# A convolution-and-attention chain on one core: three of 24 depthwise chains move to TensorE

## The chip, the cores and the metric

The kernel runs on one core of one Trainium2 chip. The metric is the device time of one execution in microseconds (us). Every time below comes from runs of the kernel before the change: three timed runs, and one execution that the hardware profiler recorded.

## The reference

Four layers run one after the other on x of shape (4, 256, 64, 64), float32, each on a group-normalised input and added to its own input. Layer 0 is a deformable convolution with a feed-forward part, layer 2 a 3x3 convolution with binarised weights, layer 3 a non-local attention block with 2x2 max pooling. The change lies in layer 1, a linear attention with a depthwise 5x5 convolution:

```python
qkv = relu(conv1x1(x, qkv_w) * qkv_bn_scale + qkv_bn_bias)       # 768 channels
agg = depthwise5x5(qkv, agg_dw_w) + agg_dw_b                      # 768 channels, 25 taps each
agg = agg * agg_pw_w + agg_pw_b                                   # per channel
t = concat([qkv, agg]) split into heads of q, k, v (8 rows each)
q, k = relu(q), relu(k)
out = (v k^T) q / (sum_n(k) . q + eps)
out = relu(conv1x1(out, proj_w) * proj_bn_scale + proj_bn_bias)
x = x + out
```

Layer 3, of which the image before it runs in the same stretch of time, is

```python
s = softmax(theta(x)^T phi(maxpool(x)));  x = x + wz(s g(maxpool(x))) + x_normalised
```

## The kernel before

**Images in a pipeline.** The four images go through the layers one behind the other. While one image's deformable convolution gathers (`sample`), the image before it does its feed-forward part and its linear attention (`feedforward`, `layer1`), and the one before that its 3x3 convolution and its attention (`layer2`, `layer3`). After the last gather comes the tail, in three steps of `run` (from L1218):

1. `feedforward(3)`, and then `layer1(3)` beside `rest`, which is `layer2(2)` and after it `layer3(2)`. Here `self.alone` and `self.spare` are set.
2. `layer2(3)` beside what is left of `rest`.
3. `layer3(3)` by itself, in the form called `wide`.

**Who sets the order.** The works are Python generators that yield a cost; `beside` runs through a number of steps and advances each work until its spent cost reaches its share of a given total. The totals are constants: `LAST = 624` for `layer1(3)`, `SECOND = 568` for `rest`, over the shares 0.27 to 1 and 0.27 to 1.05 of the steps. They don't delay anything on the chip; they only fix in which order the instructions of the works stand in each engine's queue, and each engine runs its queue in that order.

**Linear attention, `layer1`.** The 768 channels are six tiles of 128, taken as three pairs (`tiles` in `rows`), and the 64 rows of the image as four blocks of 16. Each combination of tile and block is a chain: 25 taps over a padded tile `pad` of 20 x 68. There are 24 chains. `rows` makes the padded tiles with 1x1 convolutions on TensorE (L821) that ScalarE moves to SBUF; `chains` hands out chains whose padded tile is ready, and makes more where none is.

In the tail a chain is computed in one of two ways:

- `aggregate`: 25 instructions on VectorE (`depthwise`, L178 and L180), each a multiplication by a column of weights and an addition, 128x1024, in a PSUM accumulator `agg`; the last tap writes an SBUF tile.
- `products`: 25 multiplications on ScalarE (L196, 128x1024, three buffers) and 24 additions on GpSimd (L200), in SBUF, into a tile `av2` of three buffers.

A group takes three chains: one by `products`, and two by `aggregate`, one after the other. The products advance by one with every second tap (`step`, through `aside`). Eight groups make 24 chains. `step` also pops one entry of `later` at every second tap: the work that waits for finished chains, in an order written by hand.

For the first two pairs of tiles (k and v) that work is `outer`: transposes (L870, L871), a copy by ScalarE (L875) and products that add up in the PSUM tile `vk` (L879). For the third pair (q) it is `output`: denominators (L921), their inverse on VectorE (L925, L926), for eight heads a spreading of the inverse by TensorE (L934) and a scaling on VectorE (L938), then the projection (L943), ScalarE's activation (L947) and VectorE's addition (L951). An output needs both chains of its block. What is left of `later` after the last group is popped one entry per step of cost 2.

**The attention beside it, `layer3`.** 32 tiles of 128 pixels in sequence: two score matmuls of 128x512 (L1185); their maxima on VectorE (L1186, L1187); two exponentials on ScalarE (L1191); eight transposes in two PSUM tiles (L1197) that ScalarE copies (L1199); eight matmuls (L1203); a reciprocal on VectorE (L1206); a scaling on ScalarE (L1208). After each four tiles there are two more matmuls, with the result (L1213 to L1215).

**PSUM.** A pool `mm` of three banks turns round among all short users (`self.ps`). Other banks have names: `acc` and `dp` (after the last gather used by the convolution of image 2, through `self.long`, and by the two halves of the score in `layer3(2)`), `vk`, and `agg` of two banks.

Of the kernel before, what the change touches and what calls it, by code (L numbers as in the profile page):

```python
# [9 lines left out]
F32 = mybir.dt.float32  # L10
# [7 lines left out]
P = 128  # L18
# [20 lines left out]

CONVOLVE, OFFSETS, BINARY = NB * 9 + 26, 60, 62  # L40
FEED = NB * 40 + 8
LINEAR, LAST = 938, 624
STEPS = 900
CONV, SECOND = NB * 22.5 + 11, 568
EPS_BN = 1e-5
# [26 lines left out]
class Net:  # L72
# [684 lines left out]
    def layer1(self, n, st, st2):  # L757
# [3 lines left out]
        with tc.tile_pool(name=f"la{n}", bufs=1, side="right") as sp, \  # L761
# [10 lines left out]
            ld = sp.tile([P, 4, 2, 32], F32, name="ld")  # L772
            nc.vector.memset(ld, 0.0)

            later, count, aside = [], 0, None
            alone = self.alone
            room = lambda bufs, more=1: bufs + more * alone

            def step(cost, chains=False):


                nonlocal count
                count += chains
                if later and (not alone or count % 2 or not chains):
                    later.pop(0)()
                if chains:
                    if count % 8 == 6 if alone else count in LEADS:
                        next(made, None)
                    if count % 2 and aside:
                        next(aside, None)  # L790
                return cost


# [56 lines left out]
            def products(pd, i, name, done, relu=True, **more):  # L850

                out = bp.tile([P, 16, W], F32, name=name, tag="av2", bufs=3)
                yield from self.products(bp, out, pd, self.w5[:, i], 5, 16, W, 0, self.b5[:, i:i + 1], lambda cost: cost)
                end(out, done, relu, **more)

            def end(out, done, relu, **more):
                if relu:
                    later.append(lambda: nc.scalar.activation(out, out, AF.Relu, **more))
                done(out)
# [110 lines left out]
            def chains():  # L970

                for _ in range(3 * NCH):
                    while not ready:
                        next(made)
                        yield None
                    t, tiles, c, pd = ready.pop(0)
                    got = {}

                    def done(i, v, t=t, c=c, pd=pd, got=got):
                        got[i] = v  # L980
                        if len(got) < 2:
                            return
                        if t == 2:
                            return output(c, pd, [got[0], got[1]])
                        outer(t, 1, fl(got[0]), fl(got[1]), False, c == NCH - 1)
                        if c == NCH - 1:
                            later.append(partial(summed, t))

                    for i, m in enumerate(tiles):
                        more = {} if t == 2 or i else {"accum_out": ks[t][:, 1, c:c + 1]}  # L990
                        yield pd[i], m, ("ak", "av")[i], partial(done, i), t == 2 or not i, more
# [15 lines left out]
            while number < 6 * NCH:  # L1007
                count = 0 if not alone and number % 2 == 0 else count
                *args, more = yield from chain()
                if alone:  # L1010

                    *slow, smore = yield from chain()
                    aside = products(*slow, **smore)
                    yield from aggregate(*args, **more)
                    *args, more = yield from chain()
                    yield from aggregate(*args, **more)
                    for _ in aside:
                        pass
                    number += 3
                else:  # L1020
                    yield from aggregate(*args, **more)
                    number += 1
            while later:
                yield step(2 if alone else 4)

# [74 lines left out]
    def layer3(self, n, st, wide=False):  # L1100
        nc, tc, a = self.nc, self.tc, self.a
        M = HW // 4
        with tc.tile_pool(name=f"na{n}", bufs=1, side="left") as sp, \
# [69 lines left out]
            for b in range(NB):  # L1173
                m2 = bp.tile([P, 512], F32, name="m2")
                for j in range(4):
                    if not wide and not self.spare:
                        s = [self.ps("s") for _ in range(2)]
                    elif wide and j % 2:
                        s = self.ps1.tile([P, 2, 512], F32, name="s", tag="agg")
                        s = [s[:, i] for i in range(2)]  # L1180
                    else:
                        s = [self.ps1.tile([P, 512], F32, name="s", tag=tag) for tag in ("acc", "dp")]
                    mx = bp.tile([P, 3], F32, name="mx3")
                    for i in range(2):
                        nc.tensor.matmul(s[i], tv[:, 4 * b + j], ph[:, i * 512:(i + 1) * 512], start=True, stop=True)  # L1185
                        nc.vector.tensor_reduce(mx[:, i:i + 1], s[i], AX.X, ALU.max)  # L1186
                    nc.vector.tensor_scalar(mx[:, 2:3], mx[:, 0:1], mx[:, 1:2], -1.0, ALU.max, ALU.mult)  # L1187
                    yield 1.5
                    pe = bp.tile([P, M], F32, name="pe")
                    for i in range(2):  # L1190
                        nc.scalar.activation(pe[:, i * 512:(i + 1) * 512], s[i], AF.Exp, bias=mx[:, 2:3])  # L1191
                    yield 2
                    pT = bp.tile([P, 8, P], F32, name="pT")
                    for i in range(2):
                        pt = self.ps("pt").rearrange("p (m t) -> p m t", t=P)
                        for m in range(4):
                            nc.tensor.transpose(pt[:, m], pe[:, (4 * i + m) * P:(4 * i + m + 1) * P], self.ident)  # L1197
                        yield 1
                        nc.scalar.copy(pT[:, 4 * i:4 * i + 4], pt)  # L1199
                    yield 1  # L1200
                    ps = self.ps()
                    for m in range(8):
                        nc.tensor.matmul(ps[:, 0:P + 1], pT[:, m], gt[:, m], start=m == 0, stop=m == 7)  # L1203
                    yield 1.5
                    rden = bp.tile([P, 1], F32, name="rden")
                    nc.vector.reciprocal(rden, ps[:, P:P + 1])  # L1206
                    yield 1.5
                    nc.scalar.activation(m2[:, j * P:(j + 1) * P], ps[:, 0:P], AF.Copy, scale=rden)  # L1208
                yield 1.5
                r = self.block(bp, self.x5_d[n], b, "r5", bufs=1)  # L1210
                for k in range(KT):
                    ps = self.ps()
                    nc.tensor.matmul(ps, ww[:, k * P:(k + 1) * P], m2, start=True, stop=True)  # L1213
                    nc.scalar.activation(r[:, k], r[:, k], AF.Identity, bias=bi1[:, k:k + 1], scale=sc1[:, k:k + 1])
                    nc.vector.tensor_tensor(r[:, k], r[:, k], ps, ALU.add)  # L1215
                nc.sync.dma_start(self.out[n, :, b * 512:(b + 1) * 512].rearrange("(k p) s -> p k s", p=P), r)
# [167 lines left out]
```

## Time and profile before

| | |
|---|---|
| three timed runs | 8691.39 us median, 8685.18 to 8699.55 |
| the profiled execution | 8695.07 us, of which the profile's span is 8693.3 |
| mean granted TensorE clock over the span | 0.803 |
| feed-forward of image 3 ends, linear attention begins | 7463 us |
| convolution of image 2 ends | about 7740 us |
| first of the 32 attention tiles of image 2 (L1186) | 7851 us |
| last tap on VectorE | 8196 us |
| last projection of image 3 (L943) | 8266 to 8273 us |
| convolution of image 3 (L1085) | 8307 to 8490 us |
| attention of image 3, to the end | 8490 to 8693 us |

Busy time of the engines in the whole span: TensorE 68%, VectorE 55%, ScalarE 41%, GpSimd 57%.

A profile of this kind has several views. The busy time by stretches counts how long each engine had an instruction running; matmuls overlap at their ends, so TensorE's busy time is no measure of how near it is to its peak. The groups put together all instructions of one line, engine and tile: busy time, mean nanoseconds of one, and the idle time of the engine before them with what ended it. The waits say who waited for whom: total microseconds, times, longest. The chain of waits follows the time back from the last instruction. L178 is line 178 of the kernel before. DVE is VectorE, ACT ScalarE, POOL GpSimd, PE TensorE and PEld its weight loads; the "granted clock" is the share of TensorE's full clock that the chip allowed.

### The profile page before, as it was taken

Reading aid. Unit: us, or ns where it says so; the run is one execution under the profiler, and the core shown is the slowest. Engines: PE = TensorE matmul, PEld = TensorE weight load, DVE = VectorE, ACT = ScalarE, POOL = GpSimd, SP = SyncE. Lnnn points to the kernel's source line nnn. Section 1 sums busy time; section 2 is a strip of 40 time slices with the busy share of each in tenths; the row PEclk is TensorE's granted clock in tenths of the full one; section 3 lists DMA queues with packets and bytes.
Section 4 is the critical chain, followed back from the end, with each engine's and each line's share of the span. In section 5 each row is a group of like instructions: output and inputs, shape, how many; then the busy total and the mean of one; then the engine's idle time right before and its main releaser. Section 6 shows DMA issues by size and latency. Waiting matters only on the chain.

```text
span 8693.3 us, 99761 instructions
## 1 busy us (share of the span) xinstructions
PE 5880.0 (68%) x35776; PEld 3498.6 (40%) x35776; DVE 4817.7 (55%) x6045; ACT 3541.0 (41%) x10767; POOL 4934.7 (57%) x4870
## 2 busy tenths in 40 slices
PE   4454554448744446688876676888766778986899
PEld 2232222224323222234644443345544333664476
DVE  5344442443366667324776675228766762699833
ACT  2333333234444433334445443444454442456414
POOL 2666666466666666666666556666655560476410
PEclk7676766669866667799988887999878879998899
DMA  6454554444533334444543344445433342220131
GB/s 172 129 160 123 145 149 118 114 143 148 158 107 106 110 109 126 137 127 138 142 133 111 111 116 138 146 135 142 141 105 111 112 118 96 74 72 29 44 97 54
DMA packets 744383, 1031.75 MB, mean 119 GB/s; under 512 B 354128, under 2 KB 459984, under 8 KB 742352
## 3 DMA queue, kind: packets, MB, share of 16 engines
q0 software_dynamic: 221184, 604.27, 24.4%
q1 hardware_dynamic: 522704, 421.10, 16.4%
q8 instruction: 283, 4.64, 0.2%
q14 instruction: 212, 1.74, 0.1%
HBM read 856.39 MB, written 168.61 MB: 118 GB/s over the span
## 4 chain that ended last, share of the span: by engine, by line
PE 43%; another core or an unknown queue 17%; DVE 17%; ACT 13%; issue 8%; DMA 1%; POOL 0%; SPq 0%; ACTq 0%; DVEq 0%; POOLq 0%
DVE agg L178 10%; PE acc L603 6%; PE ps L739 5%; PE ps L749 5%; ACT wm L588 5%; PE ps L1085 4%; PE ps L821 3%; PE ps L943 2%; PE ps L1203 2%; PE s L1185 2%; PE po L636 2%; ACT dT L623 2%; ACT at L608 1%; PE rden L934 1%
## 5 line engine op out<-in xcount | busy, mean ns | idle before, releaser
L596 POOL DMA_INDIRECT g<-tab,sl x4608 | 4399.0, 955 | 2790.8 <-issue 1179.7
L178 DVE SCALAR_TENSOR_TENSOR agg<-pad,vec,agg 128x1024 f32<-128x1024 f32 x2280 | 2934.5, 1287 | 63.9
L603 PE MATMUL acc<-g,wm 128*32 128x128 f32 x18432 | 1012.4, 336 | 2022.6 <-ACT at L608 1471.8
L603 PEld LDWEIGHTS acc<-g,wm 128*32 128x32 f32 x18432 | 557.7, 129 | 2524.7 <-ACT at L608 1683.4
L588 ACT ACTIVATE wm<-sl,con 128x48 f32<-128x48 f32 x6144 | 1490.1, 366 | 26.0 <-remote 12.6
L1085 PE MATMUL ps<-xd,w 128*128 128x256 f32 x3072 | 741.0, 392 | 37.6 <-issue 30.1
L623 ACT COPY dT<-dp 64x128 f32<-64x128 f32 x1152 | 297.2, 258 | 985.8 <-remote 524.3
L1085 PEld LDWEIGHTS ps<-xd,w 128*128 128x128 f32 x3072 | 587.3, 196 | 159.0 <-issue 79.0
L739 PE MATMUL ps<-x2f,f 128*128 128x512 f32 x1024 | 502.3, 639 | 10.2 <-issue 5.1
L608 ACT COPY at<-acc 128x256 f32<-128x256 f32 x576 | 214.5, 372 | 712.8 <-remote 607.4
L821 PE MATMUL ps<-xr,qw 128*128 128x512 f32 x768 | 463.5, 733 | 21.8 <-issue 8.5
L724 DVE SCALAR_TENSOR_TENSOR hm<-ps,vec,lk 128x512 f32<-128x512 f32 x256 | 190.6, 750 | 502.4 <-ACT lk L741 375.2
L749 PE MATMUL ps<-hm,f 128*128 128x512 f32 x1024 | 463.6, 601 | 0.0
L741 ACT ACTIVATE lk<-ps,low 128x512 f32<-128x512 f32 x256 | 174.0, 687 | 514.7 <-PE ps L739 413.2
L636 PE MATMUL po<-dT,ow 128*128 128x288 f32 x1024 | 336.7, 477 | 56.5 <-issue 13.8
L875 ACT COPY kt<-pt 128x512 f32<-128x512 f32 x256 | 149.5, 585 | 544.8 <-remote 246.8
L1036 POOL TENSOR_TENSOR xd<-xp 128x640 f32<-128x640 f32 x64 | 79.8, 1275 | 497.3 <-DMA xq<-x 280.3
L1203 PE MATMUL ps<-gt,pT 128*128 128x129 f32 x2048 | 316.5, 315 | 47.1 <-ACT pT L1199 32.9
L613 PE MATMUL dp<-ident,at 128*128 128x128 f32 x1152 | 285.5, 336 | 77.1 <-ACT dT L623 53.4
L1203 PEld LDWEIGHTS ps<-gt,pT 128*128 128x128 f32 x2048 | 297.2, 226 | 98.8 <-ACT pT L1199 45.0
L1185 PE MATMUL s<-ph,th 128*128 128x512 f32 x512 | 289.2, 677 | 42.9 <-DVE ot L938 9.2
L739 PEld LDWEIGHTS ps<-x2f,f 128*128 128x128 f32 x1024 | 199.2, 203 | 253.3 <-issue 238.5
(243 smaller groups left out, 7710.6 us busy)
## 6 DMA issues: line engine op xcount, KB each, us to landing
g<-tab,sl POOLq DMA_INDIRECT x4608
x<-x SPq DMA_DIRECT2D x128, 512.0 KB
xr<-x SPq DMA_DIRECT2D x96, 512.0 KB
tab<-xo SPq DMA_DIRECT2D x192, 128.0 KB
x<-in_x SPq DMA_DIRECT2D x32, 512.0 KB
y<-yc SPq DMA_DIRECT2D x32, 512.0 KB
yb<-y SPq DMA_DIRECT2D x64, 256.0 KB
x<-yb SPq DMA_DIRECT2D x64, 256.0 KB
```

Of the source, the lines that this page charges most:

```text
L178: nc.vector.scalar_tensor_tensor(to, s, wt, acc, ALU.mult, ALU.add)
L588: nc.scalar.activation(wm[:, :, :, o], blocks[b][:, r:r + WR, G:], AF.Copy, scale=self.con("own")[:, o:o + 1])
L596: nc.gpsimd.indirect_dma_start(out=g[:, i, :], out_offset=None, in_=table, in_offset=bass.IndirectOffsetOnAxis(ap=sl.bitcast(I32)[:, r, i: ...
L603: nc.tensor.matmul(acc[32 * i:32 * i + 32, :], wm[:, r4, 4 * i + 2 * x:4 * i + 2 * x + 2, :], g[:, i, x * P:(x + 1) * P], start=x == 0, st ...
L623: nc.scalar.copy(dT[b][hs, :, r:r + UR], dp[u][hs, :, :, s, :].rearrange("p v g o -> p g v o"))
L636: nc.tensor.matmul(po[m][:, 0:BR * OB], self.ow[:, k, m * P:(m + 1) * P], dT[b][:, k].rearrange("p r o -> p (r o)"), start=k == 0, stop=k ...
L739: nc.tensor.matmul(ps, f1[:, k, m * P:(m + 1) * P], x2[:, k], start=k == 0, stop=k == KT - 1)
L749: nc.tensor.matmul(ps, f2[:, k, m * P:(m + 1) * P], hm[:, k], start=k == 0, stop=k == 4 * KT - 1)
L821: nc.tensor.matmul(ps, qw[:, k, m * P:(m + 1) * P], x[:, k], start=k == 0, stop=k == KT - 1)
L1085: nc.tensor.matmul(ps[:, e], w[:, k, t, 2 * half + e, m * P:(m + 1) * P], v[:, 2 * half + e, k, t:t + 8], start=i % 6 == 0, stop=i % 6 == 5)
L1185: nc.tensor.matmul(s[i], tv[:, 4 * b + j], ph[:, i * 512:(i + 1) * 512], start=True, stop=True)
L1203: nc.tensor.matmul(ps[:, 0:P + 1], pT[:, m], gt[:, m], start=m == 0, stop=m == 7)
```

## The change

A third way to compute a chain is added, `diagonal`. For each tap, ScalarE multiplies the identity matrix by the column of 128 weights, which gives a diagonal matrix of 128x128 (four buffers `dg`), and TensorE multiplies it with the shifted window of the padded tile and adds up the 25 taps in PSUM. A PSUM bank holds 512 columns, so a chain is done in two halves of eight rows, and the diagonals are made anew for the second: 50 matmuls of 128x512, 50 diagonals. ScalarE then takes each half out of PSUM with bias and, where it is wanted, rectification. The diagonals run two ahead of the matmuls. The bank is `dp`.

The chain `third` advances by one matmul with every tap on VectorE, over 50 taps. The first begins in the fifth group, before its second chain on VectorE; it is used up before the second chain of the sixth, where the next begins. In the last group (`final`) what is left of that is drained in one go before the group's first tap, and the third begins there. Groups one to four take three chains and groups five to seven take four: seven groups, 14 chains on VectorE, seven by products, three by diagonals.

Since `dp` is taken, `layer3(2)` takes its second score bank from the pool `mm`. The constant `LAST` is 586 instead of 624.

```diff
-LINEAR, LAST = 938, 624
+LINEAR, LAST = 938, 586
...
                     if count % 2 and aside:
                         next(aside, None)
+                    if third:
+                        next(third, None)
                 return cost
...
+            def diagonal(pd, i, name, done, relu=True, **more):
+
+                out = bp.tile([P, 16, W], F32, name=name, tag="av2", bufs=3)
+                func = AF.Relu if relu else AF.Identity
+                left = None
+                for h in range(2):
+                    ps = self.ps1.tile([P, 512], F32, name="dg", tag="dp")
+                    made = []
+                    for t in range(25 + 2):
+                        if t < 25:
+                            made.append(bp.tile([P, P], F32, name="dg", tag="dg", bufs=4))
+                            nc.scalar.activation(made[t], self.ident, AF.Copy, scale=self.w5[:, i, t:t + 1])
+                        if t == 2 and left:
+                            left()
+                        if t > 1:
+                            y, x = divmod(t - 2, 5)
+                            nc.tensor.matmul(rw(ps), made[t - 2], pd[:, 8 * h + y:8 * h + y + 8, x:x + W], start=t == 2, stop=t == 26)
+                            yield
+                    left = partial(nc.scalar.activation, out[:, 8 * h:8 * h + 8], rw(ps), func, bias=self.b5[:, i:i + 1], **more)
+                yield
+                left()
+                done(out)
+
...
-                        next(made)
+                        next(made, None)
...
-                    aside = products(*slow, **smore)
+                    aside, final = products(*slow, **smore), number == 20
+                    if final:
+                        *then, tmore = yield from chain()
+                        for _ in third:
+                            pass
+                        *last, lmore = yield from chain()
+                        third = diagonal(*last, **lmore)
                     yield from aggregate(*args, **more)
-                    *args, more = yield from chain()
-                    yield from aggregate(*args, **more)
+                    number += 3
+                    if final:
+                        number += 1
+                    else:
+                        for _ in third or ():
+                            pass
+                        *then, tmore = yield from chain()
+                        third = None
+                        if number >= 15:
+                            *last, lmore = yield from chain()
+                            number, third = number + 1, diagonal(*last, **lmore)
+                    yield from aggregate(*then, **tmore)
                     for _ in aside:
                         pass
-                    number += 3
...
+            for _ in third or ():
+                yield step(1)
             while later:
                 yield step(2 if alone else 4)
...
-                        s = [self.ps1.tile([P, 512], F32, name="s", tag=tag) for tag in ("acc", "dp")]
+                        s = [self.ps1.tile([P, 512], F32, name="s", tag="acc")]
+                        s.append(self.ps1.tile([P, 512], F32, name="s", tag="dp") if wide else self.ps("s"))
```

More of the change, by code (lines that the diff above doesn't have):

```diff
@@ L773, in layer1 @@
             nc.vector.memset(ld, 0.0)
-            later, count, aside = [], 0, None
+            later, count, aside, third = [], 0, None, None
             alone = self.alone
```

## The prediction, made before the changed kernel ran

> **What bounds the kernel now.** I began with the busy time by stretches of time, because the change touches only the end of the program. Columns: stretch, its length, then busy microseconds (and instructions) of TensorE's matmuls, of its weight loads, of VectorE, ScalarE, GpSimd, then the granted TensorE clock, DMA share, GB/s.
>
> ```profile
> 7463.00:7740.00 277.00, 262.76 (x1216) 207.58 (x1216) 240.15 (x301) 168.57 (x238) 212.63 (x106) 0.96 0.28 77
> 7740.00:7853.00 113.00, 73.30 (x276) 45.98 (x276) 103.03 (x129) 55.49 (x83) 64.08 (x27) 0.75 0.20 65
> 7853.00:8190.00 337.00, 241.75 (x883) 141.66 (x882) 313.40 (x339) 192.49 (x263) 213.87 (x91) 0.83 0.11 36
> 8190.00:8275.00 85.00, 80.47 (x283) 43.39 (x282) 38.74 (x62) 26.58 (x43) 4.58 (x2) 0.94 0.13 44
> 8275.00:8303.00 28.00, 20.27 (x81) 15.39 (x82) 10.17 (x32) 13.53 (x21) 0.00 (x0) 0.74 0.69 227
> 8303.00:8490.00 187.00, 181.45 (x849) 157.74 (x849) 57.05 (x130) 22.42 (x33) 39.89 (x32) 0.98 0.27 78
> ```
>
> The tail's linear attention (the "linear stage") runs from 7463 to 8275. Call the rows A (beside the convolution of image 2), B (its attention begins), C, D (only the last outputs are left), then the gap and conv(3). In A both TensorE and VectorE are full; in B and C VectorE is (93% in C), while TensorE's clock is 0.75 to 0.83; in D, TensorE. Next the groups of that stretch and who waits in C:
>
> ```profile
> L178 DVE SCALAR_TENSOR_TENSOR agg<-pad,vec,agg 128x1024 f32<-128x1024 f32 x368 | 473.2, 1286 | 8.9
> L196 ACT ACTIVATE m<-pad,vec 128x1024 f32<-128x1024 f32 x192 | 219.4, 1160 | 5.2 <-POOL av L200 5.2
> L1208 ACT ACTIVATE m<-ps,rden 128x128 f32<-128x128 f32 x29 | 10.6, 366 | 78.6 <-DVE rden L1206 78.6
> ```
> ```profile
> ACT pe L1191 <- DVE mx L1187: 60.4, 21, 8.9
> PEld pt L1197 <- ACT pe L1191: 55.7, 22, 7.2
> PE pt L1197 <- ACT pe L1191: 40.8, 15, 6.5
> ```
>
> The taps (L178) are VectorE's work, and TensorE's idle time in C is mostly the wait for the softmax's exponentials, which themselves wait behind taps. So work taken off VectorE is worth its time in B and C only until another engine is full. Last, TensorE's true price, from the chain of waits, where it runs without a gap (start, length, line, records):
>
> ```profile
> 7402.38 13.73 PE ps L739 x32
> 8348.78 133.40 PE ps L1085 x618
> 8213.62 1.79 PE ps L1203 x16
> ```
>
> 13.73 / 32 = 0.429 us for a record of 512 columns, 133.40 / 618 = 0.216 for 256, 1.79 / 16 = 0.112 for 129. Each float32 matmul is two records (L739 issues 512 matmuls in the program and has 1024 records), a transpose one. A 512-wide matmul therefore costs 0.858 us at full clock, not the 0.6 mean that the groups show (records overlap).
>
> **The change, part by part.** I counted both programs' instructions in issue order from the end of feedforward(3) to the last projection (L943), and multiplied by such prices.
>
> VectorE loses two chains of 25 taps: 50 x 1.32 us (six taps took 7.91) = 66 us; one attention tile more comes in (two maxima and two short ones, 1.6). Sum 715 to 652 us. GpSimd loses one chain, 24 x 2.38 = 57 us; it was already idle between sums, so nothing. ScalarE loses 25 products (29 us) and two rectifications (2.1) and gains 150 diagonals and six evictions (6 x 0.78 = 4.7, from rows of 128x512 off PSUM). No row has a 128x128 scaling from SBUF: above it lies L1208's 366 ns (same size, from PSUM), below it the step of about 0.26 from that L1208 to the next start. I take 0.33, nearer the first: 50 us (39 to 55). Sum 477 to 503 us.
>
> The Trainium skill, "ScalarE: Activation LUTs", section "What ACT_TABLE_LOAD costs", speaks against many small activations: each pays a fixed time, 280 ns + 0.833 ns per element with one pointer operand, less 93 ns of overlap back to back. L1208 agrees roughly (366 against 387). By the page 150 diagonals would cost 150 x 0.294 = 44 us, by the row 55, an estimate either way; it leaves the sum alone, since ScalarE doesn't decide it.
>
> TensorE gains 150 matmuls x 0.858 = 129 us, and one tile (4.8). Sum 547 to 680 us. This is the heart of it: 66 us of VectorE are bought with 129 us of TensorE, all of it in the second half of the stage, because A has no diagonals.
>
> Now by stage. I cut at the attention tiles (the pair of L1185), and for each tile took the larger of TensorE's and VectorE's work, but at least 10.8 us (a tile with nothing beside it: 8275.21 to 8286.00 from one L1187 to the next). Before, tiles 1 to 21 give 326 us (nearly all VectorE; C took 337, factor 1.035), tiles 22 to 27 give 77 (TensorE; D took 85, factor 1.10). After:
> - Tiles 1 to 3, no diagonal yet: 37 us, VectorE, x 1.035 = 38.
> - Tiles 4 to 20, the diagonals: TensorE 278, VectorE 235, ScalarE 216; tile by tile the larger gives 289. The bound changes hands. One block of 27 diagonals (the rest of the second chain, drained before the last group) makes tile 14 alone 32.8 us of TensorE. Factor between the two above, 1.06: 306.
> - Tiles 21 to 28, only outputs: 99, x 1.10 = 109. There are eight rather than six, because VectorE is through with the taps three tiles earlier, but the outputs of the last two blocks still have to come.
>
> Sum 453 against 422: 31 us longer for one tile more. Set against it: LAST 586 slows linear attention against image 2's work, so that A and B hold fewer taps: VectorE 346 to 327 us, TensorE 296 to 290. A is full on both, so it gains between 4 and 13 (TensorE's and VectorE's sums for it fall by 3.5 and 13.3), I take 5; B is VectorE's at 91%, 5.6 less work is 6 to 7. Together -12. And the tile done early saves 4.8 us of conv(3)'s stretch, where TensorE is 97% busy: -5, and it costs nothing else there.
>
> What hides or doesn't: the second score bank moves from a bank of its own to the three shared ones. The users between a score and its exponential are one or two, so three suffice: 0, and if not, 1 us for each of 28 tiles. Each second half of a diagonal chain waits until ScalarE has emptied the bank: three diagonals and an eviction, 1.8 us, less TensorE's other work; six boundaries, 0 to 6 us in all, inside the factor. Queued behind on TensorE are the tile's transposes, and VectorE and ScalarE wait for those. No DMA is added; SP's queue only shifts.
>
> Sum: +31 - 12 - 5 = +14. The profiled execution took 8695.07 (span 8693.3 and 1.8 outside), which gives 8709; the median of the runs is 3.7 lower: 8705.
>
> The clock is the term with most doubt. TensorE's records in C are slowed to 0.83. At that clock 129 us would be 155, and the whole of tiles 4 to 20 278 / 0.83 = 335. In D, where TensorE has 90% of the work, it ran at 0.94 and in conv(3) at 0.98, so I price at full clock and leave the rest to the factors. The Trainium skill, "TensorE: Matmul & The Clock Gate", section "What's actually happening", says the clock is half after an idle window of about 3.4 us and whole after as long a busy one. The trace's means between are then mixtures; by the rule tiles 4 to 20 stay whole, and my 306 would stand.
>
> **The rivals.**
> 1. Likeliest, 50%: TensorE takes VectorE's place, 8705, own range 8688 to 8722 (the factor 1.06 for tiles 4 to 20 between 1.00 and 1.12, 289 x 0.06 = 17 each way).
> 2. Faster, 27%: the queues run ahead, so no tile pays its own maximum. For: in A, from 7500 to 7740, TensorE and VectorE were both 96% busy. Against: there nothing chained them to each other at every tile. Then tiles 4 to 20 cost TensorE's 278 x 1.03 = 286 and D's factor falls to 1.03 (102): 38 + 286 + 102 = 426, +4 - 17 = -13; with A's other bound (13 for 5), -21; and with the floor hidden in D (89 for 99), -31: 8660 to 8678, say 8668.
> 3. Slower, 23%: a new wait, TensorE on ScalarE's diagonals. Only two are made ahead (1.7 us of matmuls); ScalarE waits in order for L1187 (60.4 us, 21 times, 2.9 each), and the diagonals behind it come late. For: ScalarE has 216 us in 306. Against: those needed before the transposes are issued ahead of the exponential. At 2 us for each of 17 tiles, +34 on rival 1: 8739. It decides once waits for the diagonals pass 20 us.
>
> That the change doesn't do what it says is out: the issue order has 14 chains on VectorE, seven on GpSimd, 150 diagonal matmuls.
>
> **How the numbers follow.** 0.2% is 17 us, about what a measurement tells from nothing: same is 8674 to 8709. Of the likeliest case 0.32 lies in it and 0.18 above; rival 2 gives faster 0.25, same 0.02; rival 3 slower 0.22, same 0.01. So 0.25, 0.35, 0.40. The range takes in the faster case's middle part and the slower one's: 8655 to 8745, about one in ten beyond each end.
>
> **What would show it.** TensorE over 90% busy at a clock over 0.93 between the first and the last diagonal (step: the bound changes hands); 300 records of the new matmul at 0.43 apart; VectorE waiting on L1185 for over 30 us there; the last projection 10 to 25 us later than 8272; conv(3) unchanged at about 182 us. A last projection before 8255 speaks for rival 2; over 20 us of TensorE's waits on the diagonals, for rival 3. A clock at 0.85 in that stretch would make it wrong in a way that none of them has: 278 / 0.85 = 327 for 289, 8745.

## The result, and the profile after

The changed kernel takes 8728.56 us in the median of six runs (8721.98 to 8746.39), against 8695.47 for the kernel before in the runs beside it (8685.18 to 8707.84). The ratio is 1.0038, its 95% interval 1.0025 to 1.0051: 33 us slower, where 14 had been forecast. The number lies in the range, on the side (slower) that had the largest chance.

The profiled execution of the changed kernel is the longest of its six (8746.39), and the excess lies ahead of the code that was changed: the feed-forward of image 3 ends 22 us later in it. So in what follows the tail is counted from the last instruction of that feed-forward (L727 on VectorE; 7457.4 us in the profile of before, 7479.4 in that after). The two timelines give (the convolution of image 2 is taken at the start of its last addition on VectorE, the first tile at the start of L1187 of before, which is L1230 after, the convolution of image 3 from its first start to its last end; the other rows are ends):

| us from the end of feedforward(3) | before | after | difference |
|---|---|---|---|
| convolution of image 2 ends | 282.7 | 267.9 | -14.8 |
| first attention tile of image 2 | 395.6 | 367.8 | -27.8 |
| last tap on VectorE | 738.7 | 715.4 | -23.3 |
| last projection of image 3 (27 and 28 tiles by then) | 815.4 | 846.0 | +30.6 |
| convolution of image 3 | 849.5 to 1024.8 | 877.1 to 1052.5 | +27.6, +27.7 |
| end | 1235.9 | 1264.6 | +28.7 |

The stage begins 28 us earlier and gives back 58 between the first tile and the last projection. The busy time by stretches, cut as before the change by the clock of its own profile (columns: stretch, length, then TensorE's matmuls, weight loads, VectorE, ScalarE, GpSimd, granted clock, DMA share, GB/s):

```profile
7463.00:7740.00 277.00, 268.34 (x1228) 210.58 (x1227) 227.79 (x303) 158.61 (x224) 202.04 (x101) 0.97 0.28 81
7740.00:7847.00 107.00, 67.69 (x269) 41.49 (x267) 97.66 (x133) 56.08 (x85) 60.92 (x26) 0.81 0.22 69
7847.00:8180.00 333.00, 299.24 (x1070) 166.76 (x1071) 245.13 (x273) 211.98 (x381) 165.50 (x70) 0.95 0.09 29
8180.00:8330.00 150.00, 136.27 (x471) 72.35 (x469) 67.38 (x105) 47.03 (x79) 9.61 (x5) 0.93 0.14 48
8330.00:8355.00 25.00, 16.84 (x68) 12.45 (x68) 7.30 (x27) 12.51 (x20) 0.00 (x0) 0.73 0.73 244
8355.00:8540.00 185.00, 178.81 (x828) 156.07 (x829) 55.77 (x126) 19.11 (x28) 40.20 (x32) 0.97 0.27 79
```

The third row answers to C: VectorE, 93% busy there before, is at 74%; TensorE has gone from 72 to 90%, and its clock from 0.83 to 0.95. The bound has changed hands. The fourth row answers to D and is 150 us long, where D was 85. The groups of the stretch from 7460 to 8400 (columns: line, engine, operation, tiles and shapes, count; busy us, mean ns; idle time before them and its cause):

```profile
L178 DVE SCALAR_TENSOR_TENSOR agg<-pad,vec,agg 128x1024 f32<-128x1024 f32 x322 | 413.9, 1285 | 7.7
L196 ACT ACTIVATE m<-pad,vec 128x1024 f32<-128x1024 f32 x168 | 192.4, 1157 | 2.4 <-POOL av L200 2.4
L874 PE MATMUL dg<-pad,dg 128*128 128x512 f32 x300 | 150.3, 621 | 12.9 <-ACT av L871 8.3 <-ACT dg L869 4.6
L869 ACT ACTIVATE dg<-ident,vec 128x128 f32<-128x128 f32 x150 | 56.2, 397 | 25.2 <-PE dg L874 25.0
L1251 ACT ACTIVATE m<-ps,rden 128x128 f32<-128x128 f32 x32 | 11.5, 360 | 39.6 <-DVE rden L1249 39.6
```

Two chains fewer stand on VectorE (368 to 322; 23 of a chain's 25 taps carry this line and tile), and one chain of products fewer on ScalarE (192 to 168); the 300 records of the diagonal matmuls and the 150 diagonals are new. TensorE waited 12.9 us ahead of those matmuls, and only 4.6 of it for a diagonal. A diagonal takes 0.397 us, more than the 0.366 that I had as the upper end. The waits between the first tile and 8190 (who waited for whom: us, times, longest):

```profile
ACT pe L1234 <- DVE mx L1230: 57.7, 20, 8.2
...
DVE rden L1249 <- PE ps L1246: 39.3, 9, 24.7
DVE mx L1229 <- PE s L1228: 28.5, 21, 5.7
ACT dg L869 <- PE dg L874: 25.0, 30, 6.7
...
PEld dg L874 <- ACT dg L869: 12.4, 14, 3.0
...
PEld pt L1240 <- ACT pe L1234: 6.7, 7, 2.4
```

The exponentials still wait for the maxima. But the transposes that waited 55.7 us for the exponentials wait 6.7 now: TensorE has other work in front. VectorE waits for TensorE in its place (39.3 and 28.5). The chain of waits shows the price of a record (start, length, line, records):

```profile
8055.38 21.89 PE dg L874 x50
```

21.89 / 50 = 0.438 us, against 0.429 forecast. This is the block that is drained ahead of the last group; VectorE waits 24.70 us behind it for the sums of L1246, which is the longest wait of VectorE in the lines above. Last, the stage cut at the tiles that the prediction named (1 to 3, 4 to 20, 21 to 28; columns as in the stretches above):

```profile
7847.20:7885.80 38.60, 30.40 (x144) 20.79 (x144) 35.43 (x41) 28.00 (x40) 25.12 (x11) 0.90 0.09 28
7885.80:8210.40 324.60, 299.12 (x1020) 160.32 (x1020) 228.79 (x258) 195.97 (x361) 149.99 (x64) 0.96 0.08 28
8210.40:8330.00 119.60, 105.99 (x376) 58.01 (x376) 48.13 (x79) 35.04 (x58) 0.00 (x0) 0.91 0.17 56
```

The forecast had 38, 306 and 109.

### The profile page after: what moved, and what is told of

Its sections match the earlier page's. It is cut to its first block, busy times and chain, and to the rows that moved or that the text cites. A ratio compares the mean times of both kernels' runs of the same rounds, so it can differ in the third digit from the quotient of the medians.

```text
span 8744.0 us, 100396 instructions
## 1 busy us (share of the span) xinstructions
PE 6002.1 (69%) x36076; PEld 3552.1 (41%) x36076; DVE 4747.1 (54%) x5995; ACT 3564.2 (41%) x10896; POOL 4883.8 (56%) x4846
## 4 chain that ended last, share of the span: by engine, by line
PE 39%; DVE 12%; another core or an unknown queue 9%; ACT 9%; issue 4%; DMA 0%; POOL 0%; SPq 0%; DVEq 0%; ACTq 0%; POOLq 0%
DVE agg L178 8%; PE acc L603 5%; PE ps L1127 5%; PE ps L739 4%; PE ps L749 4%; PE ps L823 3%; PE ps L968 3%; PE ps L1246 3%; ACT wm L588 2%; PE s L1228 2%; PE po L636 2%; PE rden L959 1%; PE dg L874 1%; ACT dT L623 1%
## 5 line engine op out<-in xcount | busy, mean ns | idle before, releaser
L178 DVE SCALAR_TENSOR_TENSOR agg<-pad,vec,agg 128x1024 f32<-128x1024 f32 x2234 | 2875.1, 1287 | 62.6
L200 POOL TENSOR_TENSOR av<-av,m 128x1024 f32<-128x1024 f32 x120 | 284.1, 2368 | 209.6 <-ACT m L196 204.3
L1246 PE MATMUL ps<-gt,pT 128*128 128x129 f32 x2048 | 305.3, 308 | 41.6 <-ACT pT L1242 26.7
L1246 PEld LDWEIGHTS ps<-gt,pT 128*128 128x128 f32 x2048 | 289.1, 220 | 91.3 <-issue 49.1
```

The lines of the kernel that those rows point to most:

```text
L178: nc.vector.scalar_tensor_tensor(to, s, wt, acc, ALU.mult, ALU.add)
```

## The experiments

They ran where the kernel before took 7715.71, 7716.92 and 7715.89 us in three groups of runs, some 980 less than above. The difference lies ahead of the tail; the tail is the same (a kernel that is the one before but for a PSUM bank has its first tile there at 395.1 and its end at 1238.4, for 395.6 and 1235.9). The changed kernel itself was not run there; where a kernel is compared with it, that is by the tail of the profile, or by the 33 us that it stood above the kernel before.

**Half the columns of the diagonal matmuls.** Of the 25 taps of a half, 23 are computed for four rows of eight, which leaves out half of their result; order, diagonals and evictions stay.

```diff
+r = 8 if t in (2, 26) else 4
-nc.tensor.matmul(rw(ps), made[t - 2], pd[:, 8 * h + y:8 * h + y + 8, x:x + W], start=t == 2, stop=t == 26)
+nc.tensor.matmul(rw(ps)[:, 0:r], made[t - 2], pd[:, 8 * h + y:8 * h + y + r, x:x + W], start=t == 2, stop=t == 26)
```

> Of the 150 diagonal matmuls all but the first and last of each half take 256 columns instead of 512 (half the rows of the 5x5 sum are left out); every instruction stays. TensorE loses 138 x 0.43 = 59 us of work. Theory (TensorE's added work is what ends each tile in tiles 4 to 20): that stretch falls from 324 us to about VectorE's 235 with stalls, 265 to 275, so 45 to 60 us less, 8670 to 8685, below the kernel before. Rival (what costs is the wait for ScalarE's diagonals and bank evictions, which all stay): within 12 us of 8728.

Measured: 7721.53 us, ratio to the kernel before 1.0008 (0.9999 to 1.0017). The tail ends at 1231.5, 33.1 before that of the changed kernel. The groups:

```profile
L875 PE MATMUL dg<-pad,dg 128*128 128x256 f32 x276 | 78.3, 403 | 2.0 <-ACT dg L869 2.0
L869 ACT ACTIVATE dg<-ident,vec 128x128 f32<-128x128 f32 x150 | 55.8, 397 | 13.4 <-PE dg L875 12.8
```

138 matmuls became shorter by 0.429 each, 59.2 us of TensorE, and the tail fell by 33: 0.56 us for each microsecond. By the distances from the kernel before it is 27 (33 to 6). That lies between the theory's 45 to 60 and the rival's 12; tiles 4 to 20 take 292 us, not 265 to 275. TensorE's matmuls are the largest single cause, since the other parts that were tried singly (below) bring 8 us or less, but not the whole limit.

**Few diagonals.** ScalarE makes four diagonals per half and TensorE uses them over and over, which leaves out the weights of the other 21 taps; the matmuls stay.

```diff
-made.append(bp.tile([P, P], F32, name="dg", tag="dg", bufs=4))
-nc.scalar.activation(made[t], self.ident, AF.Copy, scale=self.w5[:, i, t:t + 1])
+if t < 4:
+    made.append(bp.tile([P, P], F32, name="dg", tag="dg", bufs=4))
+    nc.scalar.activation(made[t], self.ident, AF.Copy, scale=self.w5[:, i, t:t + 1])
+else:
+    made.append(made[t % 4])
```

> ScalarE makes 4 diagonals for each half of a chain instead of 25 and the matmuls use them in turn (the other taps' weights are left out): 126 activations fewer, some 45 us of ScalarE, while TensorE does the same 150 matmuls. Theory (TensorE bound; it waited 13 us in all for diagonals and evictions): 5 to 15 us less, 8713 to 8724. Rival (ScalarE's queue is the new bound): 30 us less or more, 8700 or below.

Measured: 7745.36 us, 1.0036 (1.0022 to 1.0050); the tail ends 8.4 us before that of the changed kernel. The group of what is left:

```profile
L870 ACT ACTIVATE dg<-ident,vec 128x128 f32<-128x128 f32 x24 | 8.1, 392 | 0.0
```

126 activations, 48 us of ScalarE's busy time, are gone, and 8 us of the tail. Rival 3 (TensorE waits for diagonals) is not what made the kernel slower.

**Six diagonals in flight** in place of four (`bufs=6`), nothing else.

> The changed kernel with six diagonals in flight in place of four, nothing else. ScalarE waited 25 us in the tiles for a diagonal's buffer to be read by TensorE, and TensorE 17 us for ScalarE's diagonals. The emission still makes only two ahead of their products, so a larger ring frees ScalarE but does not make a diagonal earlier in the order. My theory (the tiles' waits are a chain through all engines, of which the ring is a small part): 0 to 8 us below the changed kernel, 25 to 33 above the kernel before. Rival 3 of the prediction (ScalarE's diagonals are the wait that decides): 15 us or more below the changed kernel, under 18 above the kernel before.

Measured: 7751.56 us, 1.0049 (1.0035 to 1.0062), 35.7 above the kernel before, where the changed one stood 33 above and the expectation had 25 to 33. ScalarE's wait for a free buffer fell:

```profile
L869 ACT ACTIVATE dg<-ident,vec 128x128 f32<-128x128 f32 x150 | 55.4, 396 | 10.4 <-PE dg L874 10.4
```

From 25.0 to 10.4 us, and the tail ended at 1261.8 for 1264.6. That wait cost next to nothing.

**No block before the last group.** The second diagonal chain is not drained in one go; in the last group two matmuls go with every tap of the second chain on VectorE.

```diff
-if final:
-    *then, tmore = yield from chain()
-    for _ in third:
-        pass
-    *last, lmore = yield from chain()
-    third = diagonal(*last, **lmore)
...
-                    if third:
+                    for _ in range(1 + twice if third else 0):
                         next(third, None)
...
+        number, third, twice = number + 1, diagonal(*last, **lmore), final
```

> The rest of the second diagonal chain isn't drained in a block before the last group; it goes on beside the last group's first chain of taps, and the third chain then advances by two matmuls with every tap of the second. Same instructions on every engine. Theory (the sum of TensorE's work decides): within 10 us of 8728. Rival (the block of 27 matmuls, during which VectorE waited 24.7 us, is what made the change slower): 20 to 30 us less, 8698 to 8708.

Measured: 7747.54 us, 1.0036 (1.0023 to 1.0050); the tail ends 7.4 us earlier. Tile 14, which holds the block and took 40.2 us, takes 17.6 here, but tiles 4 to 20 together 319.8 for 324.6. The block is conspicuous in the timeline and moves the time little: the same matmuls come in other tiles.

**Two of 25 taps.** The diagonal chains compute only their first and last tap: the order, the evictions and the seven groups stay, 138 matmuls and 138 diagonals go.

```diff
+if t in (0, 24):
     made.append(bp.tile([P, P], F32, name="dg", tag="dg", bufs=4))
     nc.scalar.activation(made[t], self.ident, AF.Copy, scale=self.w5[:, i, t:t + 1])
+else:
+    made.append(None)
...
+if made[t - 2] is not None:
     nc.tensor.matmul(rw(ps), made[t - 2], ...)
```

> Of each half of a diagonal chain only the first and last tap are made and multiplied (the other 23 are left out): 12 matmuls and 12 diagonals instead of 150, evictions and order as in the changed kernel. It is the floor of seven groups, if TensorE's and ScalarE's new work were free: TensorE 118 us less, ScalarE 46. Theory (66 us of VectorE's work are worth nearly their time when nothing takes its place): tiles 4 to 20 in 245 to 265 us, 65 to 80 us below the changed kernel, 30 to 50 below before. Rival (the waits of evictions, of the output's buffers and of the longer end cost most by themselves): less than 45 us below the changed kernel.

Measured: 7701.55 us, 0.9977 (0.9967 to 0.9988): 15 us below the kernel before. The tail ends 52.7 before that of the changed kernel: less than the theory's 65 to 80, more than the rival's 45; tiles 4 to 20 take 272.7 us, not 245 to 265. Even with the three diagonal chains almost free for TensorE and ScalarE, this order of work would bring no more than that. The next experiment gives the kernel to compare it with.

**LAST alone, and the change without it.** First the kernel before with `LAST = 586`, then the changed kernel with 624.

```diff
-LINEAR, LAST = 938, 624
+LINEAR, LAST = 938, 586
```

> The kernel before, with LAST 586 instead of 624 and nothing else: only the order in which the works' instructions are queued. In the changed kernel the way to the first attention tile became 28 us shorter (368 for 396 us after feedforward(3)). Theory (the order alone does that, by putting taps off into the stretch behind, where VectorE is the bound of the kernel before, so it is paid back): first tile at +366 to +370, total within 8 us of before. Rival (the order alone is a gain that the change then loses): 20 us or more below before.

Measured: 7711.82 us, 0.9994 (0.9985 to 1.0003). The first tile starts at 368.4, as in the changed kernel (367.8): the constant by itself gives the whole gain of A and B. And it is mostly given back: the tail ends at 1221.4, 14.5 earlier than before, and the median is 5.1 lower, which the interval doesn't tell from nothing.

> The changed kernel with LAST 624 as before. Theory (taps put off cost nothing where TensorE is the bound; without that they lie in the first stretch, which VectorE bounds): 5 to 20 us slower than the changed kernel, 38 to 53 above before, first tile at +393 to +398. Rival (putting them off makes the end longer, so LAST 586 is part of the loss): at most 20 us above before.

Measured: 7759.87 us, 1.0052 (1.0039 to 1.0066), 43 above the kernel before. Its first tile is at 389.4 (6 us earlier than before the change, with the same constant), its last projection at 833.3, its end at 1267.5. So the 22 us that 586 gains at the first tile (389.4 to 367.8) are worth some 3 us at the end in the profiles, and the intervals of 1.0038 and 1.0052 overlap. At either value the change costs about as much: 43 us with 624, 38 with 586 (33 above the kernel before, whose own version with 586 is 5 below it).

Now the stretch from the first tile to the last projection, cut at the last tap, in the kernel before with 586, and below it in the one with two of 25 taps (columns as above):

```profile
6852.40:7220.00 367.60, 275.49 (x1022) 173.77 (x1023) 341.44 (x377) 216.79 (x300) 232.74 (x98) 0.82 0.11 38
7220.00:7292.50 72.50, 66.35 (x219) 32.58 (x219) 30.47 (x49) 19.69 (x32) 0.00 (x0) 0.96 0.15 51
```
```profile
6863.00:7161.00 298.00, 225.14 (x849) 139.10 (x850) 258.17 (x289) 176.92 (x257) 174.93 (x74) 0.84 0.10 32
7161.00:7288.00 127.00, 114.48 (x410) 62.17 (x410) 50.46 (x83) 36.40 (x60) 0.00 (x0) 0.93 0.16 54
```

VectorE has 63 us less to do (371.9 to 308.6), the taps end 70 us sooner, and the stretch as a whole is 16 shorter, with 28 attention tiles in it instead of 29; at the end of the tail 9.5 us are left (1221.4 and 1211.9). The other 54 went behind the last tap: 72.5 us became 127, with TensorE 90% busy there, while ahead of the last tap it was idle for a quarter of the time. TensorE's groups in those second rows show what it does:

```profile
L943 PE MATMUL ps<-ot,pw 128*128 128x512 f32 x64 | 29.0, 599 | 0.0
...
L1203 PE MATMUL ps<-gt,pT 128*128 128x129 f32 x64 | 9.3, 305 | 0.0
```
```profile
L972 PE MATMUL ps<-ot,pw 128*128 128x512 f32 x90 | 40.8, 597 | 0.0
...
L1250 PE MATMUL ps<-gt,pT 128*128 128x129 f32 x144 | 22.2, 318 | 1.9 <-ACT pT L1246 1.9
```

90 records of the projections remain after the last tap instead of 64, and nine attention tiles (16 records of L1250, or L1203, each) instead of four. The instructions stand in that order in TensorE's queue: the projections come off `later` at every second tap or after the last, the tiles by their cost, and neither moves forward when VectorE is through sooner. So the time taken off VectorE came back as TensorE's work at the end. That the order in the queue is what holds it there is read from these counts and from the program; no run changed that order alone (a version that takes two entries of `later` at a time, for instance).

**The second score bank alone.** The kernel before with the score bank taken from `mm`, as in the change.

```diff
-s = [self.ps1.tile([P, 512], F32, name="s", tag=tag) for tag in ("acc", "dp")]
+s = [self.ps1.tile([P, 512], F32, name="s", tag="acc")]
+s.append(self.ps1.tile([P, 512], F32, name="s", tag="dp") if wide else self.ps("s"))
```

> The kernel before with one of the change's parts alone: the second score bank of the last image's attention comes from the three shared banks, not from a bank of its own. My theory, as the prediction priced it: nothing, within 5 us of the kernel before, since one or two users stand between a score and its exponential and three banks suffice. Rival: the score waits for a bank in each of the 28 tiles, 1 us each, so about 28 us longer.

Measured: 7717.58 us, 1.0001 (0.9992 to 1.0011). Nothing that the interval tells from zero, as forecast.

**Fewer chains on TensorE.** Eight groups, each with a chain of products, as before; two chains of 24 by diagonals, or one. Groups five and seven (or seven alone) start one, and the group after each has a single chain on VectorE.

```diff
+for group in range(8 if alone else 0):
+    *args, more = yield from chain()
+    *slow, smore = yield from chain()
+    aside, single = products(*slow, **smore), group in (5, 7)
+    yield from aggregate(*args, **more)
+    if not single:
+        *then, tmore = yield from chain()
+        if group in (4, 6):
+            *last, lmore = yield from chain()
+            third = diagonal(*last, **lmore)
+        yield from aggregate(*then, **tmore)
...
-                    if count % 2 and aside:
+                    if (count % 2 or single) and aside:
```

The version with one has `(7,)` and `(6,)` in place of the two pairs. Two, with LAST 586:

> Eight groups again, eight chains by products, 14 on VectorE, only two by diagonals (beside groups five and six, seven and eight; groups six and eight have one chain on VectorE). Against the changed kernel TensorE has 43 us less, GpSimd 57 us more, VectorE the same. Theory (a third of TensorE's added work only relieved GpSimd, which bounds nothing): 30 to 50 us less, 8680 to 8700, faster than or level with before. Rival (the diagonals cost by their waits and by the reordering, not by TensorE's sum): 8715 to 8730; or GpSimd becomes the bound in the two short groups: above 8730.

Measured: 7707.21 us, 0.9986 (0.9977 to 0.9995): 8.5 below the kernel before, 42 less than the changed kernel by their distances from it, as the theory had it. One, with LAST 605:

> One chain by diagonals (beside groups seven and eight; group eight has one chain on VectorE), 15 on VectorE, eight by products, LAST 605. Against before: VectorE 33 us less, TensorE 43 more. Two chains gave 11 us below before. Theory (a chain by diagonals is worth 33 us of VectorE as long as TensorE has room, and the second meets less room than the first): 5 to 20 us below before, at least level with two chains. Rival (the gain comes from the count of chains off VectorE, TensorE still having room at two): half of two chains' gain, 3 to 7 below before.

Measured: 7737.03 us, 1.0026 (1.0016 to 1.0037), which neither theory had (and two chains had given 8.5 us, not the 11 of the expectation). Its first tile came at 386.7, not 368.4, so I tried the constant by itself:

```diff
-LINEAR, LAST = 938, 605
+LINEAR, LAST = 938, 586
```

> The version with one chain of 24 on TensorE, which came out 20 us slower than the kernel before with LAST 605, with LAST 586 alone changed. My theory: LAST cost most of that. In the run with 605 the first tile began 18 us later after the end of feedforward(3) than in the version with two chains and 586 (386.7 against 368.4), while the tiles up to the last projection took 444.0 against 434.5 there and 440.1 in the kernel before with 586. So about 18 us less than with 605: 2 us above to 5 us below the kernel before. Rival: the tile part pays for the earlier start, as half of the gain was paid back in the kernel before with 586 (28 us earlier at the first tile, 14 at the end), and it stays 8 us or more above the kernel before.

Measured: 7696.71 us, 0.9975 (0.9965 to 0.9984): 19 us below the kernel before, the fastest of all the kernels that compute the whole, and 40 below its own twin with 605, twice what I had expected. 18 of the 41.5 us of the two tails lie ahead of the first tile, another 18 between it and the last projection (444.0 to 425.8, with 28 and 29 tiles). Two chains with LAST 548:

> The version with two chains of 24 on TensorE and LAST 548 in place of 586. Theory 1: the beginning is bound by VectorE's and TensorE's work there, so each taps' work moved later starts the first tile earlier again (about 15 to 25 us), and the tiles pay back half: 5 to 12 us below the version with 586, about 16 to 22 below the kernel before. Rival: the tiles, where TensorE is now as full as VectorE, pay back all of it or more: not below the version with 586.

Measured: 7728.54 us, 1.0016 (1.0007 to 1.0025), 21 above its twin with 586. The first tile came 5 us earlier only (363.3), and the stretch to the last projection took 463.0 for 434.5 (with 29 tiles for 28). So 586 lies between two worse values, 605 and 548, each tried with one of the two versions. I know which stretches got longer, not which meeting of instructions in the queues did it.

With LAST 586, then, from the first tile to the last projection:

| chains on TensorE | TensorE busy | VectorE busy | length | tiles in it | end of the tail | median against before |
|---|---|---|---|---|---|---|
| 0 | 341.8 | 371.9 | 440.1 | 29 | 1221.4 | -5 |
| 1 | 362.0 | 342.5 | 425.8 | 29 | 1207.2 | -19 |
| 2 | 383.1 | 312.6 | 434.5 | 28 | 1217.1 | -9 |
| 3 (the change; one group less) | 431.7 | 309.5 | 478.2 | 28 | 1264.6 | +33 |

The best of the four is the one in which the two engines come nearest to being equal. That this is the reason is not shown: `LAST` alone moved the version with one chain by 40 us, more than the first three rows differ by, and no version was tried at more than two values. Its two stretches, cut at the last tap:

```profile
6856.00:7177.00 321.00, 262.04 (x976) 153.14 (x977) 292.42 (x326) 217.41 (x326) 222.22 (x94) 0.90 0.10 33
7177.00:7282.00 105.00, 100.00 (x367) 51.94 (x366) 50.10 (x77) 36.27 (x58) 10.67 (x5) 1.00 0.19 66
```

VectorE is 91% busy up to the last tap and TensorE 82%; after it TensorE has 95% at full clock. The third chain of the change took nothing more off VectorE than the second (309.5 for 312.6): it replaced a chain of products, and GpSimd, which adds these up, had been waiting anyway (119 us for ScalarE's products in C before the change).

## Why the prediction was right, and where its sizes were wrong

The likeliest case, TensorE takes VectorE's place, is what happened. Three of its five signs came: TensorE over 90% busy at over 0.93 (92% at 0.96 in tiles 4 to 20), records at 0.43 us (0.438), and the convolution of image 3 unchanged (175.3 and 175.4 from its first matmul to its last). Two came near: waits of VectorE on the scores of over 30 us (28.5, with 39.3 on the sums beside them), and a last projection 10 to 25 us later (30.6). The time itself, 33 us above the kernel before, is some 2.5 us beyond the upper end of that case's own range (8722, 30.6 above), on the way to rival 3's 8739; that it isn't rival 3 is known by the waits and by the run with few diagonals, and that it is TensorE's matmuls by the run with half their columns, which takes 27 to 33 us off.

| term of the sum | forecast | measured |
|---|---|---|
| tiles 1 to 3 | 38 | 38.6 |
| tiles 4 to 20 | 306 | 324.6 |
| tiles 21 to 28 | 109 | 119.5 |
| the same stretch before | -422 | -422.1 |
| A and B, by LAST | -12 | -27.8 |
| one tile less beside the convolution | -5 | -4.0 |
| sum | +14 | +28.8 |

The measured terms add up to the 28.7 us of the two tails. The median says 33 (22 to 44 by the interval), which agrees with it.

- **Tiles 4 to 20, the step that failed most.** The price of the matmul and the count were right, and so was the clock, which I priced full: 278 / 0.96 = 290 us. TensorE was busy 299 of the 324.6. What I took too low is the factor for waits, 1.06 over the 289 of the tile-by-tile sum; it was 1.12, the upper end of the likeliest case's own range. 8.3 us of the 25.5 idle ones are three waits at a change of halves, where the next matmul waits until ScalarE has emptied the bank (I had 0 to 6 for all six). One of the three costs 4.2 because the emptying itself stands 3.6 us behind VectorE: its `av2` buffer is still read by an output (L963). That wait was not tried by itself.
- **Tiles 21 to 28.** 1.21 over the 99 of the sum instead of 1.10. With two of 25 taps they take 117.8, nearly the same, so it is not the diagonals that did it. TensorE is busy for 106 of the 119.6 us there, with the attention and the outputs that stand at the end of its queue.
- **LAST.** I took 5 for A, within 4 to 13, and it brought 14.8; B 13.0 for 6 to 7. The tiles were forecast 30 us too short and A and B 16 us too long, and it is luck that these errors run against each other: the total is 15 off. That the gain of LAST is paid back later was not in the working: without the change it is 27 us at the first tile and 5 in the median, with the change 22 and, by the tails, 3.
- **The diagonals on ScalarE.** 0.397 us each, above my upper end of 0.366; in a row they start some 0.29 apart (in the timeline four take 1.26). The prediction says that no row has a 128x128 scaling from SBUF, but the profile before the change has one, with a column as scale, from SBUF to SBUF (groups of ScalarE over the whole span):

```profile
L1133 ACT ACTIVATE gw<-gw,g_r 128x128 f32<-128x128 f32 x8 | 2.8, 392 | 0.2 <-PE ps L1124 0.2
```

Its 0.392 us was the price to take. The figures of the Trainium skill that the prediction gave, "ScalarE: Activation LUTs", section "What ACT_TABLE_LOAD costs", come to 0.387 and 0.294, and were nearer than the two rows that I chose between. It changes little here: with 126 of the 150 gone, the tail is 8 us shorter.

- **The bank** cost nothing (1.0001). **Rival 3** is out by its own mark: 4.6 us of matmuls and 12.4 of weight loads waited for diagonals, under 20. **Rival 2** is out, too: tiles 4 to 20 took 324.6, not its 286.

What the working did not ask is what the relief of VectorE is worth by itself. It set 66 us of VectorE against 129 of TensorE. The runs show that the first, with nearly all of the second and of the diagonals left out, brings some 10 us over the kernel before with the same LAST (7701.55 and 7711.82, with intervals that just overlap; 9.5 by the tails), and that 138 of the 150 matmuls with their diagonals cost 53 in the changed kernel (the tails of 1264.6 and 1211.9).

## What to carry to other kernels

Work that goes from a full engine to one with gaps can fill the second, and then costs more than it saves. Three chains of 24, with TensorE 92% busy in tiles 4 to 20, made this kernel 33 us slower; one made it 19 faster, or 14 against the kernel before with the same `LAST`. That the best point is where both engines are equally full fits the four kernels here, but isn't shown. Before moving it, ask what the relieved engine's next limit is: here 54 of the 70 us that the taps ended sooner came back behind the last tap, as work in the other engine's queue. And a constant that sets the interleaving can be worth as much as the change (40 us between 605 and 586), so a change is to be compared with the kernel before at the same value, and the value tried anew.

## What the runs showed that I had not expected

The part ahead of the tail took about 980 us less where the experiments ran than where the first runs did, with the same instructions, while the tail agreed to 3 us. A constant that orders only the tail moved the time by 40 us in one version (605 and 586) and by 21 in another (586 and 548), while the work stayed the same; in the kernel before it moved it by 5 (624 and 586), which the interval doesn't tell from nothing.

And the added work raised TensorE's clock. In the changed kernel TensorE is 92% busy between 7890 and 8190, and the granted clock there is 0.96; before the change it was 72% and 0.82. With two of 25 taps, the same order without most of the matmuls, the like stretch is back at 75% and 0.83:

```profile
6905.00:7161.00 256.00, 192.28 (x697) 116.56 (x698) 218.99 (x245) 145.13 (x212) 146.57 (x62) 0.83 0.10 33
```

The records of the score matmul in these three stretches took 708 ns on average before, 592 after and 619 with two taps (groups of TensorE, in this order):

```profile
L1185 PE MATMUL s<-ph,th 128*128 128x512 f32 x72 | 41.6, 708 | 0.0
```
```profile
L1228 PE MATMUL s<-ph,th 128*128 128x512 f32 x64 | 30.1, 592 | 0.0
```
```profile
L1232 PE MATMUL s<-ph,th 128*128 128x512 f32 x64 | 32.1, 619 | 0.8 <-DVE r L1262 0.8
```

So 27 of the 116 ns of that shortening came with the matmuls and their higher clock; the other 89 came without them, at a mean clock near that of before. Part of those came with `LAST` alone (657 ns in the kernel before with 586, from 6890 to 7220); what the rest comes from the runs don't show. The 138 matmuls that tell the two later kernels apart are 118 us by the price of 0.858, but TensorE's busy time from the first tile to the last projection differs by 92 (339.6 and 431.7, with 28 tiles in both).
